# Fold products over four PSUM banks, weight loads issued first, and a reordered start of the first image

## The chip, the cores and the metric

The kernel runs on one NeuronCore of a Trainium2 chip. The metric is the device time of one execution in microseconds. Five runs of the kernel before took 671.73 to 672.25 us, with a median of 672.01 us.

The engines are named as the profile names them: PE is TensorE (PEld is its weight load), DVE is VectorE, ACT is ScalarE, POOL is GpSimd, and SP is SyncE, which here only issues transfers. PSUM is the memory that TensorE writes its products to; it has banks of 512 fp32 words for each partition.

## The reference

The input `x` is 4 images of 256 channels and 64 x 64 pixels, in fp32. Two layers follow each other. The first computes weights for 49 shifted copies of an image from the image itself, and sums the copies with these weights:

```python
k = conv(x, w1, padding=6, rhs_dilation=2) + b1       # w1: 128 x 256 x 7 x 7
k = conv(k, w2) + b2                                  # w2: 49 x 128 x 1 x 1
attn = softmax(k, axis=1)                             # over the 49 shifts
shifts = stack([xp[:, :, 2*u:2*u+64, 2*v:2*v+64] for u in range(7) for v in range(7)], axis=1)
x = einsum('bkchw,bkhw->bchw', shifts, attn)
```

The second whitens the channels in 4 groups of 64: mean and covariance over all images and pixels, five Newton-Schulz steps on the 64 x 64 covariance, the product with the centred data, then gain and shift for each channel.

## The kernel before

Nothing non-linear stands between the two convolutions, so the kernel multiplies their weights first: `w2 * w1` is one 7 x 7 convolution from 256 channels to 49 maps, and `w2 * b1 + b2` its bias. I call this product the fold. Channels come in two halves of 128 (`cc` in the code, `NCC = 2`).

**The prologue.** SP's queue issues, in program order: w2 (line 169), b1 (171), b2 twice (175), then w1 in five pieces for each half of the channels (`w1_sb`, line 215; pieces of 30, 30, 30, 20 and 18 channels), then the first image (225), then gain and shift (233, 234). The first image comes in 16 loads of 256 KB. It is split by row parity (`pr`, one buffer for each), by half of the channels, and by phase `a`, the row number modulo 4 within a parity; the order of the phases is 3, 0, 1, 2.

TensorE transposes w2 (182), DVE copies it twice into `w2T` (184), and a product with b1 (186) gives the bias (188). Then the fold follows: 13 blocks of 10 channels (the last of 8). A block is one fp32 product for each half (line 251, 490 columns, written to partitions 0 to 48 and 64 to 112 of one PSUM bank), and one eviction of both (`evict`, line 244). The profile shows an fp32 product as two records, which I call passes. Blocks alternate between the two banks `cv_buf`, and evictions between ACT (even blocks) and DVE (odd blocks). The evicted fold lies with output maps on partitions; 49 transposes (269), in 13 groups of 4 in the `tp` banks, turn it to have channels on partitions, and the same `evict` moves each group to `tap`, again by turns of ACT and DVE.

**The convolution.** It is done in the manner of Toom-Cook (Winograd) in both directions. Rows and columns are split into four phases, and weights and image are evaluated at seven points in each direction (`ROWS`, `BANKS`). The point 0 and the point at infinity of the rows are done as direct convolutions (`direct`, line 779), the others as products of evaluated weights and evaluated image (`conv_bank`, line 604), whose results are interpolated on DVE.

For the first image the order of the work on DVE is written out by hand (`in_turn`, `strict`): each DVE instruction is kept behind the one before in the program. The part that matters here is: `row_weights(1)` adds weight taps (into `lgx`, then `gbr`), `weights` evaluates them for the columns into `wr`, `row_eval(0, 1)` adds image phases (0 + 2 into `rb[0]`, 1 + 3 into `rb[1]`, for each parity, then both into `rb[2]`), and `col_ops` evaluates the columns into `ct` and `xh`. At the same time TensorE does `direct0(INF, 0)`, which reads phase 3 of the image, and `direct0(0, 0)`, which reads phase 0; then it begins with `conv_bank` for rows of point 1, which reads `wr` and `xh`. Program order on TensorE is kept by `pe(...)`.

**Behind it.** The other three images follow in the same way, with softmax, the weighted sum of shifted pixels (products with `band` matrices that go through DRAM, lines 1158, 1208 and 1328), and the covariance sums (`sig`, line 1419) in planned gaps between convolution steps. The tail computes the whitening matrix and writes the output (lines 1730 to 1872). `acc` (line 820) are two more PSUM banks, of the pool that later holds the weighted sums; DVE clears them (822) and the direct convolutions of the first image write to them. `diag` and `cmask` (117 to 126) are small constants for the softmax.

These lines are `evict`, the loop of the fold and the sums of phases in `row_eval`:

```python
    def evict(k, o, i):
        (nc.vector.tensor_copy if k % 2 else nc.scalar.copy)(o, i)

    for k, c0 in enumerate(range(0, P, CB)):
        n = min(CB, P - c0)
        t = cv_buf[k % 2]
...
            if br == 1:
                add(r[0], xs[:, 0], xs[:, 2])
                add(r[1], xs[:, 1], xs[:, 3])
```

Of the kernel before, what the change touches and what calls it, by code (L numbers as in the profile page):

```python
# [32 lines left out]
def kernel(  # L33
# [75 lines left out]
    def tp():  # L109
# [8 lines left out]
    diag = const.tile([P, SW + 2 * R], F32, name="diag")  # L118
    nc.gpsimd.memset(diag, 0.0)
    nc.vector.tensor_reduce(  # L120
        diag[:, R : R + SW], ident.rearrange("p (j w) -> p w j", w=SW), AX.X, ALU.add
    )
    cmask = const.tile([P, KS], F32, name="cmask")
    for v in range(KS):
        nc.vector.tensor_reduce(
            cmask[:, v : v + 1], diag[:, KS - 1 - v : KS - 1 - v + SW], AX.X, ALU.add
        )
# [41 lines left out]
    nc.sync.dma_start(w2_sb, w2.rearrange("k o a b -> k (o a b)"))  # L169
# [10 lines left out]
    nc.gpsimd.memset(w2T, 0.0)  # L180
    t = tp()
    nc.tensor.transpose(t[:O1, :KT], w2_sb, ident[:KT, :KT])
    for h in range(2):
        nc.vector.tensor_copy(w2T[:, h * HB : h * HB + KT], t[:O1, :KT])
    t = tp()
    nc.tensor.matmul(t[:, :1], w2T, b1_sb, start=True, stop=True)
    bias = const.tile([P, 1], F32, name="bias")
    nc.vector.tensor_tensor(bias, t[:, :1], b2_sb, ALU.add)

    cv_buf = []  # L190
    for k in range(2):
        t = ps_cv.tile([P, 512], F32, name=f"cv{k}")
        nc.vector.memset(t, 0.0)
        cv_buf.append(t)
    sig = ps_sg.tile([P, NCC, GW + 1], F32, name="sig")

# [9 lines left out]
    w1_sb = [w1p.tile([O1, P, KT], F32, name=f"w1_{cc}") for cc in range(NCC)]  # L206

# [3 lines left out]
    CB = 10  # L211
    for c0, c1 in ((0, 3), (3, 6), (6, 9), (9, 11), (11, 13)):
        c0, c1 = c0 * CB, min(c1 * CB, P)
        for cc in range(NCC):
            nc.sync.dma_start(
                w1_sb[cc][:, c0:c1].rearrange("o c t -> o (c t)"),
                w1[:, cc * P + c0 : cc * P + c1].rearrange("o c u v -> o (c u v)"),
            )
# [27 lines left out]
    for k, c0 in enumerate(range(0, P, CB)):  # L246
        n = min(CB, P - c0)
        t = cv_buf[k % 2]
# [11 lines left out]
        )  # L260
    every = [u * KS + v for u in UPOS for v in range(KS)]
    flat = tap.rearrange("p u v a k -> p (u v) a k")
    TB = 4
    for k0 in range(0, KT, TB):
        n = min(TB, KT - k0)
        t = tp()
        for k in range(n):
            pe(
                nc.tensor.transpose(  # L269
                    t[:, k * P : k * P + K2], tapT[:K2, every[k0 + k]], ident[:K2, :K2]  # L270
                )
            )
# [215 lines left out]
    def row_eval(b, br, rb=rb):  # L488

        for pr in range(2):  # L490
# [329 lines left out]
    acc = [ps_y.tile([P, Q8, W], F32, tag="y", name=f"acc{sr}") for sr in range(2)]  # L820
    for a in acc:
        nc.vector.memset(a, 0.0)
# [1083 lines left out]
```

## Time and profile before

| what | value |
| --- | --- |
| runs, median (lowest to highest) | 672.01 us (671.73 to 672.25) |
| the profiled execution | 677.36 us |
| its span, from first to last instruction | 675.6 us |
| PE busy | 648.5 us, 96% of the span |
| DVE busy | 566.5 us, 84% |
| ACT busy | 333.1 us, 49% |
| POOL busy | 115.3 us, 17% |
| DMA | 126.09 MB, 187 GB/s in the mean |
| mean granted TensorE clock | 0.989 |

The profile of one execution answers several questions. The page gives busy shares, the span in 40 slices of 16.9 us (each digit is a busy share in tenths), and the chain of work that ended last, followed back from the end. A row of the timeline has its start in us, its duration, the engine, the source line, the operation with the tile that it writes and those that it reads, the shape, and the number of merged instructions; in brackets stand the idle time before it and what ended it. A row of the waits reads: who waited, for whom, us in total, times, longest. A row of the table by stretches has the stretch, its length, then busy us (and the number of instructions) of PE, PEld, DVE, ACT and POOL, then the granted clock of TensorE as a share of full speed, the busy share of the DMA engines and GB/s. Where no clock event is recorded before a stretch, the table shows 1.00.

### The profile page before, as it was taken

To read this page: it belongs to the slowest core of one execution; us is meant where nothing else is said; L and a number is where in the kernel's file an instruction comes from. 1 tells how busy PE (TensorE), PEld (TensorE's weight loads), DVE (VectorE), ACT (ScalarE), POOL (GpSimd) and SP (SyncE) were. 2 spreads that over 40 slices of the span, in tenths; PEclk is the share of its full clock that TensorE was granted. 3 is DMA by queue.
4 is the path that set the end of the run, shared out by engine and by line. 5 is a ranking of instruction groups with operands and counts; after the bars stand their busy time and mean duration, and the time that the engine had idled before them with its cause. 6 is when DMAs were issued, how large, how long until landed. Compare 5 with 4: busy or idle time off the path is not lost.

```text
span 675.6 us, 19064 instructions
## 1 busy us (share of the span) xinstructions
PE 648.5 (96%) x7800; PEld 529.1 (78%) x7800; DVE 566.5 (84%) x1240; ACT 333.1 (49%) x862; POOL 115.3 (17%) x173
## 2 busy tenths in 40 slices
PE   6999999999999997999999999999999999999993
PEld 1439573357899996989999999899999999998430
DVE  3699999999399889979999879989999988633773
ACT  1424331023565564556756464455754476635663
POOL 0000551662213011000122020002130203400000
PEclk9999999999999998999999999999999999999997
DMA  8951899994599979412668594026374334749698
GB/s 315 250 166 66 134 250 370 218 191 59 118 208 223 193 260 310 120 51 80 179 221 294 173 320 120 2 67 170 105 195 117 75 71 105 193 96 383 247 405 346
DMA packets 110991, 126.09 MB, mean 187 GB/s; under 512 B 69255, under 2 KB 92344, under 8 KB 109752
## 3 DMA queue, kind: packets, MB, share of 16 engines
q1 hardware_dynamic: 94104, 69.35, 35.8%
q0 software_dynamic: 10752, 37.26, 21.4%
q10 hardware_dynamic: 6048, 18.27, 9.1%
q8 instruction: 61, 1.00, 0.6%
q14 instruction: 26, 0.21, 0.1%
HBM read 78.78 MB, written 52.36 MB: 194 GB/s over the span
## 4 chain that ended last, share of the span: by engine, by line
PE 85%; DMA 6%; DVE 5%; ACT 1%; issue 1%; SPq 0%; POOL 0%; DVEq 0%; ACTq 0%; POOLq 0%
PE cv L604 30%; PE y L1328 14%; PE cv L779 12%; PE acc L779 8%; PE sig L1419 5%; PE tp L1400 4%; PE tp L1264 4%; DMA out_dram<-out 3%; DMA slot<-in_x_dram 3%; PE cv L251 2%; PE tp L1730 1%; PE tp L1021 1%; PE tp L269 1%; DVE pv L352 1%; DMA w<-in_L_conv_w_dram 1%
## 5 line engine op out<-in xcount | busy, mean ns | idle before, releaser
L604 PE MATMUL cv<-xh,wr 128*49 128x128 f32 x4160 | 233.5, 274 | 0.1
L604 PEld LDWEIGHTS cv<-xh,wr 128*49 128x49 f32 x4160 | 227.3, 124 | 3.2 <-issue 1.0
L1158 POOL DMA_DIRECT2D sd<-zt x120 | 63.3, 534 | 300.4 <-ACT zt L1139 237.6
L1328 PE MATMUL y<-band,xb 128*128 128x209 f32 x448 | 93.7, 341 | 0.4 <-ACT xb L1295 0.4
L1328 PEld LDWEIGHTS y<-band,xb 128*128 128x128 f32 x448 | 75.7, 191 | 1.3 <-ACT xb L1295 0.6
L615 ACT COPY pv<-cv 113x486 f32<-113x486 f32 (+2 forms) x60 | 25.9, 432 | 86.6 <-PE cv L604 82.6
L352 DVE SCALAR_TENSOR_TENSOR pv<-pv 113x162 f32<-113x162 f32 x176 | 53.5, 326 | 1.5 <-ACT pv L615 0.9
L1410 ACT COPY yt<-tp 128x512 f32<-128x512 f32 x60 | 34.9, 589 | 24.8 <-PE tp L1400 23.9
L1139 ACT COPY zt<-d 32x112 f32<-32x112 f32 (+2 forms) x132 | 38.6, 292 | 11.1 <-DVE d L1009 5.7
L1400 PE MATMUL tp<-ident,slot 128*128 128x128 f32 x240 | 41.3, 296 | 0.2 <-ACT slot L1350 0.2
L1264 PE MATMUL tp<-ident,slot 128*128 128x128 f32 x256 | 40.9, 284 | 0.0
L1061 ACT ACTIVATE d<-tp,mx 128x49 f32<-128x49 f32 x96 | 27.5, 323 | 26.5 <-DVE mx L1058 19.8
L1419 PE MATMUL sig<-yt 128*64 128x65 f32 x1024 | 38.0, 225 | 0.9 <-ACT yt L1410 0.9
L1400 PEld LDWEIGHTS tp<-ident,slot 128*128 128x128 f32 x240 | 34.9, 205 | 5.1 <-issue 3.6
L1264 PEld LDWEIGHTS tp<-ident,slot 128*128 128x128 f32 x256 | 38.5, 205 | 0.4 <-DMA sd<-zt 0.4
L1419 PEld LDWEIGHTS sig<-yt 128*64 128x64 f32 x1024 | 32.9, 137 | 6.7 <-issue 1.9
L1295 ACT COPY xb<-tp 128x512 f32<-128x512 f32 x52 | 30.6, 588 | 9.1 <-PE tp L1264 6.0
L779 PE MATMUL acc<-slot,tap 128*49 128x256 f32 (+7 forms) x224 | 34.7, 468 | 0.0
L352 DVE SCALAR_TENSOR_TENSOR xh<-ct 128x512 f32<-128x512 f32 x40 | 26.6, 696 | 6.2 <-PE cv L604 5.9
L779 PEld LDWEIGHTS acc<-slot,tap 128*49 128x49 f32 x224 | 16.1, 123 | 17.9 <-issue 15.5
L147 POOL DMA_DIRECT2D slot<-in_x_dram x12 | 20.4, 1701 | 54.4 <-DVE xh L352 38.3
L348 DVE TENSOR_TENSOR pv<-pv 113x162 f32<-113x162 f32 (+1 forms) x77 | 27.8, 370 | 0.3
(258 smaller groups left out, 1143.9 us busy)
## 6 DMA issues: line engine op xcount, KB each, us to landing
out_dram<-out SPq DMA_DIRECT2D x31, 512.0 KB, 5.2
band<-sd SPq DMA_DIRECT2D x64, 242.0 KB, 3.2
sd<-zt POOLq DMA_DIRECT2D x120, 77.0 KB, 4.1
wr<-gd ACTq DMA_DIRECT2D x14, 588.0 KB, 4.2
wr<-gd ACTq DMA_DIRECT2D x14, 490.0 KB, 4.3
slot<-in_x_dram POOLq DMA_DIRECT2D x12, 512.0 KB, 10.5
ahead<-in_x_dram POOLq DMA_DIRECT2D x12, 512.0 KB, 7.5
spill<-slot POOLq DMA_DIRECT2D x3, 2048.0 KB, 8.2
```

The source lines that it names most:

```text
L348: return in_turn(TT(o, a, b, ALU.subtract))
L352: return in_turn(STT(o, a, f, b, ALU.mult, ALU.add))
L604: nc.tensor.matmul(o, wv[:, sc, sr, cc], xv[bc][:, h * NCC + cc], start=(j == 0), stop=(j == len(terms) - 1), skip_group_check=True,)
L779: nc.tensor.matmul(ps[h * HB : h * HB + KT, :, o0:o1], w[v][:, cc], rhs, start=(j == 0 and k == 0), stop=(j == len(order) - 1), skip_group ...
L1139: ins = nc.scalar.copy(o, i)
L1158: dma = queue.dma_start(bass.AP(tensor=D.tensor, offset=D.offset + h * HS + g * RS, ap=[[LS, TC], [CR * RS, NCH], [1, KS * WS]],), zt[p0 : ...
L1264: nc.tensor.transpose(t[:, h * C + cc * P : h * C + (cc + 1) * P], tile_of(xt, cc, t8, h, pc), turned_by(n),)
L1295: (nc.vector.tensor_copy if n > 4 * B - 3 else nc.scalar.copy)(xb.rearrange("p a c -> p (a c)"), t[:, : 2 * C])
L1328: nc.tensor.matmul(y_ps[n, half, cc][:, q0 : q0 + nq, c0:c1], xb[:, cc * P : (cc + 1) * P], rhs, start=(k == 0), stop=(k == len(PIECES[hal ...
L1400: nc.tensor.transpose(t[:, h * C + cc * P : h * C + (cc + 1) * P], tile_of(yt, cc, t8, h, pc), turned_by(n),)
L1410: return nc.scalar.copy(yb.rearrange("p h a g c -> p (h a g) c")[:, :, :GW], t[:, : 2 * C].rearrange("p (e c) -> p e c", c=GW),)
L1419: nc.tensor.matmul(sig[g * GW : (g + 1) * GW, cc], yb[:, g, :GW], yb[:, g], start=(count[0] == 0), stop=end, skip_group_check=True,)
```

## The change

It has six edits, all ahead of or inside the first image's start.

1. w1's loads are issued first on SP's queue, in six pieces for each half (10, 20, 30, 30, 30 and 8 channels); b1 and b2 follow them there, and w2 is issued on ACT's queue.
2. Five products of the identity with itself (`warm`) stand around the transpose of w2, and TensorE's program order now holds from there.
3. The fold rotates over four banks, `cv_buf` and `acc`. `acc` is made and cleared in the prologue for this, behind the copies of `w2T`.
4. The bias product stands behind the fold; `diag` and `cmask` are made behind the copies of `w2T`.
5. Of the 13 groups of transposes DVE evicts four (1, 3, 6 and 9), ACT nine.
6. The first image's phases are loaded in the order 3, 0, 2, 1, and for row point 1 the sums of phases 1 + 3 come behind the sums 0 + 2 of both parities.

On POOL only the clearing of `diag` moves, behind the identity. After these steps each engine has the same instructions in the same order as before.

```diff
-    nc.sync.dma_start(w2_sb, w2.rearrange("k o a b -> k (o a b)"))
+    nc.scalar.dma_start(w2_sb, w2.rearrange("k o a b -> k (o a b)"))
+    w1_sb = [w1p.tile([O1, P, KT], F32, name=f"w1_{cc}") for cc in range(NCC)]
+
+    CB = 10
+    for c0, c1 in ((0, 1), (1, 3), (3, 6), (6, 9), (9, 12), (12, 13)):
+        c0, c1 = c0 * CB, min(c1 * CB, P)
+        for cc in range(NCC):
+            nc.sync.dma_start(
+                w1_sb[cc][:, c0:c1].rearrange("o c t -> o (c t)"),
+                w1[:, cc * P + c0 : cc * P + c1].rearrange("o c u v -> o (c u v)"),
+            )
...
+    def warm(n):
+
+        t = tp()
+        for _ in range(n):
+            pe(nc.tensor.matmul(t[:, :P], ident, ident, start=True, stop=True))
+
+    warm(2)
     t = tp()
-    nc.tensor.transpose(t[:O1, :KT], w2_sb, ident[:KT, :KT])
+    pe(nc.tensor.transpose(t[:O1, :KT], w2_sb, ident[:KT, :KT]))
     for h in range(2):
-        nc.vector.tensor_copy(w2T[:, h * HB : h * HB + KT], t[:O1, :KT])
-    t = tp()
-    nc.tensor.matmul(t[:, :1], w2T, b1_sb, start=True, stop=True)
-    bias = const.tile([P, 1], F32, name="bias")
-    nc.vector.tensor_tensor(bias, t[:, :1], b2_sb, ALU.add)
+        w2_turned = nc.vector.tensor_copy(w2T[:, h * HB : h * HB + KT], t[:O1, :KT])
+    warm(3)
...
+    acc = [ps_y.tile([P, Q8, W], F32, tag="y", name=f"acc{sr}") for sr in range(2)]
+    for a in acc:
+        with tc.issue_after(w2_turned.ins):
+            nc.vector.memset(a, 0.0)
...
-    for c0, c1 in ((0, 3), (3, 6), (6, 9), (9, 11), (11, 13)):
...
-    for a in (3, 0, 1, 2):
+    for a in (3, 0, 2, 1):
...
-        t = cv_buf[k % 2]
+        t = (*cv_buf, *(a.rearrange("p q w -> p (q w)") for a in acc))[k % 4]
...
+    t = tp()
+    pe(nc.tensor.matmul(t[:, :1], w2T, b1_sb, start=True, stop=True))
+    bias = const.tile([P, 1], F32, name="bias")
+    nc.vector.tensor_tensor(bias, t[:, :1], b2_sb, ALU.add)
...
         evict(
-            k0 // TB, flat[:, k0 : k0 + n],
+            k0 // TB in (1, 3, 6, 9), flat[:, k0 : k0 + n],
...
+        odd = []
...
             if br == 1:
                 add(r[0], xs[:, 0], xs[:, 2])
-                add(r[1], xs[:, 1], xs[:, 3])
+                odd.append((r[1], xs[:, 1], xs[:, 3]))
...
+        for o in odd:
+            add(*o)
```

More of the change, by code (lines that the diff above doesn't have):

```diff
@@ L116 @@
     nc.gpsimd.tensor_copy(ident3[:, P:], ident[:, :GW])
[L118 to L127, printed above, removed]
     pivot = const.tile([P, NCC], F32, name="pivot")
@@ L194 @@
         cv_buf.append(t)
+    acc = [ps_y.tile([P, Q8, W], F32, tag="y", name=f"acc{sr}") for sr in range(2)]
+    for a in acc:
+        with tc.issue_after(w2_turned.ins):
+            nc.vector.memset(a, 0.0)
     sig = ps_sg.tile([P, NCC, GW + 1], F32, name="sig")
+    diag = const.tile([P, SW + 2 * R], F32, name="diag")
+    nc.gpsimd.memset(diag, 0.0)
+    with tc.issue_after(w2_turned.ins):
+        nc.vector.tensor_reduce(
+            diag[:, R : R + SW], ident.rearrange("p (j w) -> p w j", w=SW), AX.X, ALU.add
+        )
+    cmask = const.tile([P, KS], F32, name="cmask")
+    for v in range(KS):
+        nc.vector.tensor_reduce(
+            cmask[:, v : v + 1], diag[:, KS - 1 - v : KS - 1 - v + SW], AX.X, ALU.add
+        )
     NSK = 2 * NCC * KT
@@ L205 @@
     gb5 = gpool.tile([P, KS, NCC, 2, KT], F32, name="gb5")
-    w1_sb = [w1p.tile([O1, P, KT], F32, name=f"w1_{cc}") for cc in range(NCC)]
     tapT = w1p.tile([P, KT, P], F32, name="tapT")
-    CB = 10
-    for c0, c1 in ((0, 3), (3, 6), (6, 9), (9, 11), (11, 13)):
[L213 to L218, printed above, removed]
     for pr in range(2):
         slots[pr] = store[pr]
-    for a in (3, 0, 1, 2):
+    for a in (3, 0, 2, 1):
         for pr in range(2):
@@ L818, in direct_start @@
         direct(1, 0, sr, conv_psum(), [gr0[:, v, :, sr] for v in range(KS)])
-    acc = [ps_y.tile([P, Q8, W], F32, tag="y", name=f"acc{sr}") for sr in range(2)]
-    for a in acc:
-        nc.vector.memset(a, 0.0)
     rows = [(0, br) for br in (1, 2, 3)]
```

## The prediction, made before the result was known

> **What bounds the kernel now.** I read the page first (slices, then the chain), then the timeline of the first 60 us, the DMA rates of the first 45 us, the waits of the first 29 us, and last a table of TensorE by stretch and the chain around 250 us.
>
> ```profile
> PE   6999999999999997999999999999999999999993
> PE 85%; DMA 6%; DVE 5%; ACT 1%; issue 1%; SPq 0%; POOL 0%; DVEq 0%; ACTq 0%; POOLq 0%
> ```
>
> TensorE is the bound, and it is full nearly everywhere. It stops for long at three places: the first slice, slice 16 (a stall near 265 us) and the last one. The change works in the first. All five engines' instruction orders, before against after, differ only in the prologue (up to the first image's row sums), so what is won or lost there is handed on if TensorE stays without gaps behind it.
>
> The timeline of TensorE and of the queue that loads:
>
> ```profile
> 2.33 6.58 SPq L215 DMA_DIRECT2D w<-in_L_conv_w_dram  x10
> 6.70 15.66 PE L251 MATMUL cv<-w,w2T 128*49 128x490 f32 x52 [1.97 <-DMA w<-in_L_conv_w_dram]
> 20.68 0.17 PEld L251 LDWEIGHTS cv<-w,w2T 128*49 128x49 f32 x2 [0.16 <-DMA w<-in_L_conv_w_dram]
> 22.41 0.49 ACT L244 COPY tapT<-cv 113x392 f32<-113x392 f32 x1 [1.40 <-PE cv L251]
> 22.95 3.44 PE L269 MATMUL tp<-ident,tapT 113*128 113x113 f32 x32 [0.58 <-ACT tapT L244]
> 26.57 1.79 PE L269 MATMUL tp<-ident,tapT 113*128 113x113 f32 x16 [0.19 <-ACT tap L244]
> 28.53 0.32 PE L269 MATMUL tp<-ident,tapT 113*128 113x113 f32 x1 [0.17 <-ACT tap L244]
> 28.78 11.59 PE L779 MATMUL cv<-slot,tap 128*49 128x512 f32 x56
> ```
>
> Fold products run from 6.70 to 22.4, tap transposes to 28.8, then convolution without a gap. The third line is the one that matters: the last fold weights land at 20.68 - 0.04 = 20.64 and TensorE was already there. The waits of the first 29 us and the DMA rates (40 slices of 1.125 us):
>
> ```profile
> PEld cv L251 <- DMA w<-in_L_conv_w_dram: 4.1, 4, 2.1
> PEld cv L251 <- DVE tapT L244: 3.6, 5, 0.8
> PEld cv L251 <- ACT tapT L244: 3.3, 6, 0.7
> GB/s 0 22 1 136 397 403 408 423 413 429 418 423 418 411 429 412 405 320 232 218 218 217 218 218 228 216 193 203 214 237 228 219 189 218 145 157 389 393 392 149
> ```
>
> The eviction waits (6.9 us) look like the prize of four banks. They are not: the weights (6.42 MB) flow at about 415 GB/s from 4.1 to 19.7 without a break, so the fold is load-bound at its end, and a faster TensorE would wait for data instead.
>
> **The change part by part.**
>
> *Weights first.* The first weight load moves from 2.33 to the queue's first slot, 0.75 (where w2 is issued now): 1.58 us earlier at equal latency. In the slices data starts about 4.1, 1.8 us after issue, and w2, issued at 0.75, is used at 2.54; small b1/b2 loads now sit directly ahead, so part of the 1.8 may be theirs, which would make the gain 2.2. On the other side a first piece of 245 KB lasts 0.6 us and an issue takes 0.43 us at the median (0.33 to 0.71), so a gap of up to 0.6 us can open: gain 1.0. I take 1.7, near the plain move. w2 goes out on ACT's queue; ACT's first eviction comes only at 10.5 us, so its table load (1.28 us) behind that issue has room.
>
> *Pieces.* The last piece is 8 channels, but the one ahead has 30, and its second half decides. All lands at 20.64 - 1.7 = 18.94; the two last halves are 2 x 196 KB = 0.40 MB, 0.97 us, so the second half of channels 90 to 119 is there at 17.97. TensorE then owes blocks 9 to 12 of that half. The two halves go to separate output partitions and run side by side, so a half alone takes as long as a whole block: from the direct convolution, 56 passes in 11.59 us are 0.207 us each, 0.41 for two side by side; so 0.82 us for both passes of a 490-column block. Three blocks, then a 0.33 us pass (392 columns) and a last record of 0.49: 3 x 0.82 + 0.33 + 0.49 = 3.28. Start 18.01, end 21.29, against 22.37 now: 1.08 gained, 0.6 less than the loads gain.
>
> *Four banks.* They keep those blocks free of evictions; evictions run at 0.57 (ACT) and 0.67 (DVE), each for every second block (1.64). With two banks the same burst would wait about 0.2 us per block, so 0.5. The accumulators' memsets (1.03) move onto DVE after w2T, over 1 us before block 2.
>
> *Warm-up.* Records of 1022 to 1055 ns until 12, against 574 from 13, show half rate at the start. Two passes alone took 1.87 there (6.70 to 8.6), so five identity products of 128 columns are 5 x 1.87 x 128/490 = 2.4 us, while TensorE waits for data; the last three may hold the first block up by a microsecond: 0 at the end. A cold block costs 1.64 against 1.22 of load, so the fold may fall some four blocks behind by 10 us; it catches up at 0.82.
> The Trainium skill ("TensorE: Matmul & The Clock Gate", Part 1) says that full clock comes after a busy window of 3.4 us that runs freely, whatever the instruction count; by it the warm-up alone is too short, and the sum would stay the same, since loads set the end. "DMA: Bandwidth & Descriptors" (Specifications) puts HBM at about 358 GB/s for a core; by it the weights would need 17.9 us, but the slices show 397 to 429, and they decide.
>
> *The bias product* moves behind the fold, where TensorE waits 0.58 us for the last eviction (now two records, 0.58 at half rate): hidden, if b1, now behind the weights, has landed. It lands about 19.5, used at 21.3.
>
> *Transposes.* 13 groups of 0.39 are 5.1 us; they take 5.83 (22.95 to 28.78). Two waits of about 0.35 each (26.57, 28.53) come from ACT. Nine evictions on ACT (0.57 apart, 5.1) and four on DVE free DVE for its row sums; replaying the groups by hand with three buffers I lose about 0.25 instead of 0.7. Gain 0.45; bounds -0.3 (nine ACT evictions become the stream) and 0.7.
>
> *Image loads and sums.* 16 loads of 256 KB at 218 GB/s, 1.2 us each, follow the weights; with b1/b2 between (0.5) they move up by 1.2. Phase order 3, 0, 2, 1 and odd sums last:
>
> ```profile
> 38.16 4.63 DVE L345 TENSOR_TENSOR rb<-slot 128x1024 f32<-128x1024 f32 x4 [1.24 <-DMA slot<-in_x_dram]
> 48.22 1.23 DVE L352 SCALAR_TENSOR_TENSOR ct<-rb 128x1024 f32<-128x1024 f32 x1
> 51.57 8.68 PE L604 MATMUL cv<-xh,wr 128*49 128x128 f32 x156
> 93.22 2.29 DVE L352 SCALAR_TENSOR_TENSOR rb<-rb,rb 128x2048 f32<-128x2048 f32 x1
> 97.00 2.30 PE L779 MATMUL acc<-rb,gbr 128*49 128x512 f32 x10
> ```
>
> The 1.24 us wait goes: the even sums find their data; the last odd sum needs the 16th load, about 40.5 - 1.2 = 39.3, ends 40.5 instead of 42.8. DVE gains 2.3, but TensorE does not wait for it: xh is ready 3.4 us before 51.57. It is cover, not gain. DVE is full from 52 to 97, so this cover passes down: at 97.00 TensorE uses what DVE finished at 95.51, 1.5 us earlier. If DVE gained nothing, the first 1.5 us would still pass there.
>
> **Sum.** 1.08 + 0.45 = 1.53, with a little for the slow tail of the last load (it shares the queue with the image): 1.6. The profiled execution took 677.36 (span 675.6); it should take 675.8. The median of the runs, 672.01, lies 5.35 below that; the same loss gives 670.4. Bounds: load 1.0, transposes -0.3: 0.1; load 2.2 and 0.7: 2.4. About 0.2%, 1.3 us, is what a measurement can tell.
>
> **The place where this can change size.** At 265:
>
> ```profile
> 247.87 17.20 DMA slot<-in_x_dram
> 267.08 1.17 PE y L1328 x4
> 264.60:268.00 3.40, 0.92 (x4) 0.93 (x5) 3.23 (x6) 2.51 (x5) 0.00 (x0) 0.51 0.68 227
> 268.00:271.50 3.50, 3.50 (x30) 3.13 (x31) 3.46 (x7) 3.14 (x5) 0.00 (x0) 0.50 0.77 276
> 271.50:275.00 3.50, 3.50 (x68) 3.50 (x66) 3.43 (x7) 0.18 (x1) 0.00 (x0) 1.00 0.05 16
> ```
>
> TensorE idles 4.62 us and then works at a granted clock of 0.5 until 271.5: 4.4 us, 2.2 lost. The idle stretch moves up by 1.6 with the work. If the clock still rises at 271.5, 6.0 us run at half rate (3.0 lost, 0.8 worse); if it rises half of the 6.9 us step earlier, at 268.05, 1.3 are lost (0.9 better). I can't tell which, and the forecast leaves the loss as it is.
>
> **Rivals.**
> 1. Forecast, 670.4: 0.50; its own range 669.6 to 671.5.
> 2. The clock rises earlier behind the stall: 669.5, 0.18. For: TensorE would be busy for three quarters of that stretch instead of a quarter.
> 3. It rises at the same time: 671.2, 0.17. For: a busy half (6.70 to 8.6 of 5.2 to 8.6) did not lift it at the start.
> 4. The gain does not reach the end, or the change does not do what it says: bank waits turn into load waits, loads start no earlier, or the stall at 265, of which 17.2 us are a transfer, keeps its time: 672.0, 0.08. Against: that transfer is issued behind bands that follow TensorE's own work.
> 5. Slower: the clock stays at half through the fold's end. Then the last four blocks cost 3 x 1.64 + 0.65 + 0.82 = 6.4 instead of 3.28: -1.6 + 3.1 = +1.5, 673.5, 0.07. It decides if the clock is not up by about 14 us (five cold blocks by 12, four fast ones after, are still in time at 18). Against: cold, TensorE is slower than the loads and so never idle, as from 8.6 to 12 when it rose.
>
> **How the numbers follow.** Faster by over 0.2%: rival 1 two thirds (0.33), rival 2 nearly all (0.17), rival 3 a little (0.03): 0.53. Slower: 0.07. The rest 0.40. Range 668.7 to 672.2: from rival 2 with the better bound of the loads to rival 4.
>
> **What would show it.** First weight load at 0.75; last fold wait on a weight load at about 18, with four blocks after it; transposes from 21.9; convolution from 27.2; even row sums without a wait; first L604 about 50.0; the gap near 265 at 261 to 265.5. It is wrong if TensorE waits for DVE between 50 and 97, or if fold products still end after 22.

## The result and the profile after

The changed kernel takes 673.18 us in the median of 54 executions (671.83 to 679.38), the kernel before 671.98 us in 94 (671.62 to 678.17). The ratio is 1.0032, with a 95% interval of 1.0019 to 1.0045: **slower by 0.3%, where 670.4 was forecast.** The time is outside the range, and on the side that had 7%.

The executions of each kernel fall in two groups, and the difference has two parts. 77 of before's 94 lie at 671.62 to 672.56 us (median 671.95), 17 at 676.36 to 678.17. Of the changed kernel's 54, 31 lie at 671.83 to 674.03 (median 672.72), 23 at 677.10 to 679.38. So the changed kernel loses 0.77 us where nothing special happens, and it is in the upper group more often. Both profiled executions, 677.36 us before and 677.57 after (span 675.8), are of the upper group, so their profiles can be compared with each other, but both show a loss that most executions don't have.

The page after, TensorE's slices and the shares of the chain of work:

```profile
PE   8999999999999997999999999999999999999993
PE 82%; DMA 8%; DVE 6%; ACT 1%; issue 1%; SPq 1%; DVEq 0%; ACTq 0%
```

The first slice went from 6 to 8, though nothing became faster: the warm-up's identity products are in it. What counts is on the chain: DMA went from 6% to 8%, TensorE from 85% to 82%. The timeline of the first 53 us (start, length, engine, line, and in brackets the idle time and what ended it):

```profile
0.75 8.33 SPq L166 DMA_DIRECT2D w<-in_L_conv_w_dram  x12
4.75 1.88 PE L261 MATMUL cv<-w,w2T 128*49 128x490 f32 x4
7.49 2.34 PE L261 MATMUL cv<-w,w2T 128*49 128x490 f32 x3 [0.86 <-DMA w<-in_L_conv_w_dram]
...
19.63 0.61 PE L261 MATMUL cv<-w,w2T 128*49 128x490 f32 x1 [0.77 <-DMA w<-in_L_conv_w_dram]
...
22.89 0.38 PE L272 MATMUL tp<-b_sb,w2T 128*128 128x1 f32 x2
23.54 5.68 PE L283 MATMUL tp<-ident,tapT 113*128 113x113 f32 x49 [0.26 <-ACT tapT L254]
29.14 11.59 PE L796 MATMUL cv<-slot,tap 128*49 128x512 f32 x56
36.93 4.63 DVE L359 TENSOR_TENSOR rb<-slot 128x1024 f32<-128x1024 f32 x4
```

The loads go out at 0.75 instead of 2.33, and the first fold product starts at 4.75 instead of 6.70. But the wait for the second half of the 30-channel piece (channels 90 to 119) ends at 19.63, and the convolution starts at 29.14, 0.36 us later than before (28.78). DVE's row sums start at 36.93 without a wait (38.16 before, after 1.24 of waiting). The DMA rates of the first 45 us, in slices of 1.125 us (first the engines' busy tenths, then GB/s):

```profile
DMA  0298699999999999999999999989999999759992
GB/s 0 50 354 239 171 343 387 382 413 418 429 423 429 418 429 408 357 270 198 236 208 220 218 220 222 236 156 220 215 262 220 215 220 215 86 208 402 395 388 80
```

Data starts earlier and then falls to 239 and 171 GB/s from 3.4 to 5.6 us; it needs until 9 us to be back above 400. Before, it ran at 397 GB/s and more from 4.5 us on. This stretch uses up the whole head start. The chain of work through it:

```profile
3.08 0.43 SPq L166
...
5.81 13.78 DMA w<-in_L_conv_w_dram
19.59 0.04 issue
19.63 0.61 PE cv L261
```

The decisive piece, issued at 5.81, lands at 5.81 + 13.78 = 19.59. The slow stretch is no want of issued loads: the issue at 3.08 is the sixth, so by 3.51 loads of 3.0 MB had been issued, while by 3.4 us 0.45 MB had moved.

### The profile page after: what moved, and what is told of

The parts are those of the page before. It is cut to its first block, busy times and chain, and to the rows that moved or that the text cites. A ratio compares the mean times of both kernels' runs of the same rounds, so it can differ in the third digit from the quotient of the medians.

```text
span 675.8 us, 19093 instructions
## 1 busy us (share of the span) xinstructions
PE 651.3 (96%) x7810; PEld 531.4 (79%) x7810; DVE 566.0 (84%) x1238; ACT 333.2 (49%) x864; POOL 115.0 (17%) x173
## 4 chain that ended last, share of the span: by engine, by line
PE 82%; DMA 8%; DVE 6%; ACT 1%; issue 1%; SPq 1%; DVEq 0%; ACTq 0%
PE cv L621 30%; PE y L1342 14%; PE cv L796 12%; PE acc L796 8%; PE sig L1433 4%; PE tp L1414 4%; PE tp L1278 4%; DMA out_dram<-out 3%; DMA slot<-in_x_dram 3%; DMA w<-in_L_conv_w_dram 2%; PE tp L1744 1%; PE tp L1035 1%; SPq L166 1%; DVE pv L366 1%; PE cv L1744 1%
## 5 line engine op out<-in xcount | busy, mean ns | idle before, releaser
L1342 PE MATMUL y<-band,xb 128*128 128x209 f32 x448 | 93.7, 341 | 0.1
L1342 PEld LDWEIGHTS y<-band,xb 128*128 128x128 f32 x448 | 75.7, 191 | 1.0 <-issue 0.6
```

The costliest lines, as they stand in the source:

```text
L1342: nc.tensor.matmul(y_ps[n, half, cc][:, q0 : q0 + nq, c0:c1], xb[:, cc * P : (cc + 1) * P], rhs, start=(k == 0), stop=(k == len(PIECES[hal ...
```

## The experiments

For each run: the start of the convolution in its profile (us), the median and number of executions, the ratio to before with its 95% interval, and how many executions took over 675 us. Before has 28.78 there, the changed kernel 29.14.

| run | convolution | median, n | ratio [95%] | over 675 |
| --- | --- | --- | --- | --- |
| loads_only | 27.06 | 670.38, 9 | 0.9976 [0.9967, 0.9985] | 0 |
| after_old_pieces | 26.63 | 670.62, 11 | 0.9986 [0.9973, 0.9999] | 1 |
| after_old_loads | 28.44 | 672.09, 12 | 1.0013 [0.9998, 1.0029] | 2 |
| after_first30 | 27.27 | 671.55, 10 | 1.001 [0.9982, 1.0038] | 3 |
| after_20first | 27.67 | 671.02, 1 | | 0 |
| after_two_queues | 27.99 | 671.01, 1 | | 0 |
| after_10_30 | 28.95 | 676.08, 7 | 1.0046 [1.0025, 1.0068] | 4 |
| loads_phase | 27.58 | 670.28, 9 | 0.9977 [0.9967, 0.9986] | 0 |
| after_no_phase | 26.92 | 670.25, 12 | 0.9985 [0.997, 0.9999] | 1 |
| after_fill | 29.26 | 680.05, 6 | 1.0118 [1.0098, 1.0139] | 6 |
| after_again | 28.60 | 676.72, 1 | | 1 |
| before_again | 28.73 | 671.85, 1 | | 0 |
| after_pool_copy | 28.27 | 677.95, 9 | 1.0085 [1.006, 1.011] | 9 |
| after_early_x | 29.44 | 673.21, 10 | 1.0032 [1.0019, 1.0046] | 2 |
| loads_fine_tail | 27.06 | 670.27, 8 | 0.9969 [0.995, 0.9988] | 0 |
| best_mix | 26.11 | 670.33, 12 | 0.9991 [0.9978, 1.0005] | 0 |
| after_two_queues_timed | 28.38 | 671.20, 12 | 0.9994 [0.9975, 1.0013] | 2 |
| after_fine_tail | 26.61 | 669.82, 12 | 0.9977 [0.9957, 0.9996] | 1 |

Behind the start of the convolution, the 14 profiled executions of less than 675 us all take 641.21 to 642.11 us to the end of their span, and the four with the loss near 265 us (both kernels, after_again, after_old_loads) take 646.32 to 647.27. So where that loss is absent, the time follows the head. (after_fill and after_pool_copy, which change the work near 265 us, stand apart.)

**Is the head start lost because loads go first, or because of the pieces?** Two theories: A, a transfer that starts earlier ends no earlier, whatever the pieces; B, the new list of pieces is what moves slowly at the head.

loads_only is the kernel before with the weight loads first in the old pieces, w2 on ACT's queue and the bias product behind the fold:

```diff
-    nc.sync.dma_start(w2_sb, w2.rearrange("k o a b -> k (o a b)"))
+    nc.scalar.dma_start(w2_sb, w2.rearrange("k o a b -> k (o a b)"))
+    for c0, c1 in ((0, 3), (3, 6), (6, 9), (9, 11), (11, 13)):
...
```

> The kernel before with one edit: w1's loads first on SP's queue in the old pieces (30, 30, 30, 20, 18 channels), w2 on ACT's queue, b1 and b2 behind w1 and the bias product behind the fold. Theory A (the head start is lost in the first microseconds of the loads, whatever the pieces): the last weights still land at 20.3 to 20.7, convolution starts at 28.6 to 28.9, time within 0.3 us of before. Theory B (the small first pieces starve the DMA engines): with old pieces data runs at 400 GB/s from about 2.6, the last weights land at about 19.1, convolution starts near 27.5, and the executions are 1.0 to 1.3 us shorter than those of before of the same clock.

after_old_pieces is the changed kernel with one line edited:

```diff
-    for c0, c1 in ((0, 1), (1, 3), (3, 6), (6, 9), (9, 12), (12, 13)):
+    for c0, c1 in ((0, 3), (3, 6), (6, 9), (9, 11), (11, 13)):
```

> The changed kernel with the old pieces of w1 (30, 30, 30, 20, 18 channels). Theory A: last weights land at 20.3 to 20.7 as in both kernels, but three blocks and not four stand behind them, so the fold ends 0.6 us earlier than in the changed kernel (22.4) and convolution starts near 28.5. Theory B: last weights at about 18.9, fold ends near 20.6, convolution near 26.8, 2 us under before at the same clock.

The DMA rates of loads_only:

```profile
GB/s 0 62 248 413 423 429 423 423 434 418 423 392 422 409 404 389 204 240 222 219 230 214 221 224 223 151 222 234 236 230 225 216 213 49 346 389 392 340 6 0
```

Above 400 GB/s from the fourth slice on, without a dip; the convolution starts 1.72 us earlier than before (27.06), and the time is 1.52 us lower (670.38 against 671.90 run side by side). after_old_pieces starts it at 26.63 and takes 670.62. Theory A falls, B stands: the gain that the prediction saw in the loads is there with the old pieces. The median of after_old_pieces gains only 1.28 us of the 2 that B expected; its profiled execution, 669.95, gains them, but the ten without the loss spread over 1.0 us.

after_old_loads is the reverse: the changed kernel with before's loads, pieces and their place (the bias product stays behind the fold).

> The changed kernel with w2, b1, b2 and w1 loaded as before; four banks, warm-up products, transposes' evictions and the image's phases stay changed. Both theories: last weights land at 20.6; four banks then save at most 0.3 in the last blocks and the new split of evictions 0.2, so convolution starts at 28.2 to 28.6 and the time is 0.2 to 0.6 under before at the same clock. If the four banks or the warm-up products cost something by themselves, convolution starts after 28.8.

The convolution starts at 28.44, so the four banks and the transposes together give 0.34 us; 672.09 us can't be told from before.

**Which piece is it?** The new list differs at both ends: it begins with 10 and 20 channels, and it ends with 30 and 8 instead of 20 and 18. Four kernels take this apart; each is the changed kernel with the list, or the queue, edited:

```diff
after_first30:    ((0, 3), (3, 6), (6, 9), (9, 12), (12, 13))
after_20first:    ((0, 2), (2, 4), (4, 6), (6, 9), (9, 12), (12, 13))
after_10_30:      ((0, 1), (1, 4), (4, 7), (7, 10), (10, 12), (12, 13))
after_two_queues:
-            nc.sync.dma_start(
+            (nc.sync, nc.scalar)[cc].dma_start(
```

> The changed kernel, with its two first pieces (10 and 20 channels) joined to one of 30 as in the old list; the new end (30 channels, then 8) stays. It separates the two ends of the new list. Theory B2 (the slow head comes from the small first pieces, and the last 30-channel piece costs the 0.6 us that the prediction gave it): weight data runs at about 420 GB/s from 3 us on without the dip to 200, all weights land near 18.5 instead of 20.1, the second half of the last 30-channel piece near 18.0 instead of 19.6, fold products end near 21.4, the convolution starts near 27.2 (changed kernel 29.1, with the old pieces 26.6), and executions without the 5 us loss near 265 us take about 670.9 (old pieces 670.6, changed kernel 672.7). Rival B3 (the new end of the list is what is slow, the head only lies beside it): the dip goes, but the convolution starts at 28.5 or later and the time stays above 672.

In after_first30, the rates, and the timeline of TensorE:

```profile
GB/s 0 80 272 418 423 418 429 418 439 423 423 418 418 418 396 339 185 226 221 231 248 233 212 225 195 183 213 227 245 239 213 219 211 28 381 397 384 306 16 0
```

```profile
17.76 0.61 PE L261 MATMUL cv<-w,w2T 128*49 128x490 f32 x1 [0.75 <-DMA w<-in_L_conv_w_dram]
...
21.67 5.67 PE L283 MATMUL tp<-ident,tapT 113*128 113x113 f32 x49 [0.26 <-ACT tapT L254]
27.27 11.59 PE L796 MATMUL cv<-slot,tap 128*49 128x512 f32 x56
```

The new end is kept, the dip is gone, and the times are those of the prediction (last wait 18.01, transposes 21.9, convolution 27.2). The new end costs 27.27 - 26.63 = 0.64 us against the old pieces. Theory B2 holds, B3 falls. The median of this run is pulled up by 3 of 10 executions over 675 us and one at 674.24; the other six lie at 670.79 to 671.66.

> The changed kernel with first pieces of 20, 20 and 20 channels instead of 10, 20 and 30; for the weight data of the first 8 us only. Theory B (every piece below 30 channels moves slowly at the head): 200 to 350 GB/s until the 20-channel pieces are through, near 5 us, weights landed near 19.2, convolution near 28.2. Rival B4 (only the 10-channel first piece starts the slow stretch): no stretch below 380 GB/s after 3 us, weights landed near 18.3, convolution near 27.3.

> The changed kernel, all pieces as they are, with the loads of the second half (cc = 1) issued on ScalarE's queue behind w2 instead of all twelve on SyncE's. For the weight data of the first 8 us only. Rival B5 (the dip comes from issuing twelve loads at 0.43 us and more on one queue): the dip to 200 GB/s goes, data at 400 GB/s or more from 3 us on, weights landed near 18.3. Theory B (the packets themselves are slow at the head, 0.3 us on average and up to 1.3 for 3920 bytes against 0.15 later, while all 16 engines are busy): the dip stays, and weights land at 19.3 or later.

> The changed kernel with weight pieces of 10, 30, 30, 30, 20 and 8 channels on the one queue: the small first piece is kept, the 20-channel piece behind it is not. Theory B6 (a 10-channel first piece on one queue starts the slow stretch, whatever follows): data at 200 to 300 GB/s between 3.5 and 6 us, weights landed at 19.3 or later. Rival B7 (it takes the second small piece too): no stretch below 380 GB/s after 3.5 us, weights landed near 18.4, convolution near 26.7 to 27.2.

The rates of these three, in this order:

```profile
GB/s 0 77 273 408 418 418 404 411 437 416 418 413 423 413 410 356 204 250 212 235 202 202 247 232 195 204 205 226 235 235 223 211 224 48 193 408 344 400 127 15
```

```profile
GB/s 0 39 332 396 434 420 415 439 418 418 418 418 417 411 413 343 212 254 210 224 222 217 219 227 219 133 204 196 254 235 221 217 218 77 364 390 399 314 4 15
```

```profile
GB/s 0 52 345 286 293 335 277 387 392 429 423 423 423 413 416 404 315 242 214 197 225 204 250 225 228 191 203 172 233 269 218 219 217 213 150 2 346 397 404 323
```

Three 20-channel pieces show no dip, though twelve loads stand on one queue: what I expected of theory B ("every piece below 30 channels moves slowly") falls, and B4 holds. With the 10-channel piece first and 30s behind it, rates of 277 to 335 GB/s last until 8 us: B6 holds, B7 falls. And the changed kernel's own pieces on two queues show no dip either, as B5 said. So the slow stretch needs **a first piece of 10 channels with all loads behind it on the same queue**; either one alone doesn't do it. Why the queue is then slow for some 4 us isn't settled. The engines were busy only 8 and 6 tenths in the two worst slices of the changed kernel, and 6 tenths at 171 GB/s is less per busy engine than 9 at 418: transfers are both thinner and slower there. In after_again, the same kernel, the engines are busy throughout most of the dip, so there the packets themselves are slow:

```profile
DMA  0399979999999999999999999979899999899980
GB/s 0 61 330 275 265 268 385 382 429 423 423 418 429 423 423 413 350 250 219 224 217 218 218 218 225 223 120 214 201 263 222 226 216 217 94 343 396 394 330 8
```

By the traces' packet records, packets of 3920 bytes took 253 ns in the mean from 3.4 to 5.6 us in the changed kernel (up to 1325), 230 in after_again, and 154 in after_20first.

The Trainium skill ("DMA: Bandwidth & Descriptors", Bandwidth) advises transfers of 1 MiB and more for three quarters of the peak, beside a table of transfers issued by GpSimd. It speaks against every piece here: a half of 10 channels is 245 KB, of 20 channels 490 KB, of 30 channels 735 KB. The runs bear it out only at the smallest first piece, and there only on one queue; 490 KB pieces moved at 404 to 418 GB/s.

**Do the other edits cost something?** Executions of the changed kernel without the loss take 0.77 us more, the convolution of the profiled one starts 0.36 us later. Theory P puts the rest on the first image's phase order and sums. loads_phase is loads_only with these added; after_no_phase is after_old_pieces with them put back:

```diff
-    for a in (3, 0, 1, 2):
+    for a in (3, 0, 2, 1):
...
-                add(r[1], xs[:, 1], xs[:, 3])
+                odd.append((r[1], xs[:, 1], xs[:, 3]))
```

> loads_only (weights first in the old pieces, bias product behind the fold) with the changed kernel's order of the first image's row phases and its odd sums last. Theory P (this order brings the extra 0.4 us and the wider spread of the changed kernel's executions, by the work that DVE and the loads then do at other times): median 670.7 to 671.0 against 670.38 for loads_only, spread of 0.8 us or more, some executions 5 us longer. Rival P2 (phase order is cover and nothing else, as the prediction had it): 670.2 to 670.5, spread like loads_only's 0.5.

> after_old_pieces with the old order of the row phases and sums put back, so that the rotation over four banks, the warm-up, the split of evictions and the loads first remain. Theory P: median 670.0 or less (670.38 of loads_only less the 0.4 us by which its convolution starts earlier), spread of about 0.5 us, no execution above 672. Rival P3 (the four banks or the warm-up bring the spread): 670.5 to 670.8 and a spread of 1 us, like after_old_pieces.

670.28 against loads_only's 670.38, and 670.25 against after_old_pieces' 670.62 with overlapping executions (669.93 to 670.93 without the loss there, 669.96 to 671.00 here). In loads_phase P falls by the median: the order is neither gain nor loss, as the prediction had it; the spread, 0.80 us against 0.53, is nearer to P. For after_no_phase neither expectation is met cleanly, since the spread of 1 us stayed.

**What is lost near 265 us?** Theory C was that the clock's fall behind TensorE's wait makes the upper group, so that filling the wait would cure it. after_fill adds identity products ahead of the product that waits:

```diff
+        if m[0] == "z" and n == 2 and half == 0:
+            t = tp()
+            for _ in range(16):
+                pe(nc.tensor.matmul(t[:, :P], ident, ident, start=True, stop=True))
```

> The changed kernel with 16 products of the identity (3.4 us of TensorE, results unused) set into TensorE's order where it stands idle near 262 to 267. Theory C (the executions of either kernel fall in two groups, near 672 and near 677.5, by whether the granted clock falls in this idle stretch, and the change makes the fall more frequent): no execution near 677.5 is left, all lie at 672 to 673.2 with a mean clock of 0.994 or more. Rival D (the 5 us are a late transfer and the clock only follows): both groups stay.

It takes 677.00 to 682.12 us, five of six executions more than the median of either kernel's upper group. In the profiled execution (677.00) the fill runs from 262.10 for 3.73 us, the product behind it starts at 265.67, no longer waiting, and the clock stays at 1.00. Still it takes 645.67 us behind the start of the convolution, some 4 more than executions without the loss. So the fill costs by itself, and this run can't part C from its rival. Two more profiles of the unchanged kernels can:

> The kernel before as it is, once more, for a profile of its more frequent kind of execution (about 672.0). Theory S: convolution starts near 28.8, the gap near 265 us is about 1.1 us instead of 4.6, the load of image 2 behind the band loads is issued near 243.3 instead of 247.9, and the clock stays at 1.0 there. Rival: the gap is 4.6 us here too, so that it isn't what parts the two kinds of execution.

> The changed kernel as it is, once more, for a second profile. Theory S with theory B: if this execution takes about 672.7, the head shows the same dip to about 200 GB/s between 3.5 and 6.5 us and the convolution starts near 29, but the image-2 load near 241 to 247 us is issued earlier than 246.99, TensorE's gap near 265 is about 1.1 us and the clock does not fall there. If it takes about 678, the profile repeats the first one (gap 4.6 us, clock 0.5 until 271).

before_again took 671.85 us, one of the lower group. The stretches of before_again, and of the changed kernel (third from the end stands the granted clock):

```profile
261.00:264.60 3.60, 2.49 (x25) 2.05 (x25) 3.43 (x7) 3.54 (x6) 0.00 (x0) 1.00 0.99 372
264.60:268.00 3.40, 3.40 (x68) 3.40 (x64) 3.30 (x5) 1.94 (x4) 0.00 (x0) 1.00 1.02 382
268.00:271.50 3.50, 3.50 (x52) 3.32 (x49) 3.50 (x6) 1.98 (x5) 0.00 (x0) 1.00 0.53 147
```

```profile
261.00:264.60 3.60, 1.53 (x8) 1.20 (x8) 3.53 (x7) 0.55 (x2) 0.00 (x0) 1.00 0.96 341
264.60:268.00 3.40, 0.71 (x3) 0.71 (x4) 3.23 (x5) 2.36 (x4) 0.00 (x0) 0.50 0.62 199
268.00:271.50 3.50, 3.50 (x29) 3.13 (x30) 3.47 (x6) 3.29 (x5) 0.00 (x0) 0.51 0.74 261
```

The wait itself is most of what parts the groups, so C falls. The product with `bandz` (L1328 before, L1342 after) waits 1.11 us in before_again and 4.76 in the changed kernel's profile:

```profile
262.87 0.69 PE L1328 MATMUL y<-bandz,xbz 128*128 128x96 f32 x4 [1.11 <-ACT xbz L1286]
```

```profile
267.29 1.17 PE L1342 MATMUL y<-bandz,xbz 128*128 128x96 f32 x4 [4.76 <-ACT xbz L1300]
```

SP's queue shows where it comes from, before_again first, then the changed kernel:

```profile
232.50 2.89 SPq L482 DMA_DIRECT2D gd<-wr  x1
...
242.07 0.97 SPq L1208 DMA_DIRECT2D band<-sd  x2
243.08 0.58 SPq L147 DMA_DIRECT2D slot<-in_x_dram  x1
```

```profile
232.89 4.01 SPq L496 DMA_DIRECT2D gd<-wr  x1
...
244.86 2.09 SPq L1222 DMA_DIRECT2D band<-sd  x2
246.99 1.31 SPq L137 DMA_DIRECT2D slot<-in_x_dram  x1
```

Issues on this queue take longer in the second, and the last of the four loads of image 2's even rows goes out at 246.99 instead of 243.08. It then takes 18.35 us:

```profile
246.99 18.35 DMA slot<-in_x_dram
265.35 0.02 issue
265.37 0.04 ACTq L525
265.40 0.04 issue
265.44 0.13 ACT rb L525
```

ACT's copy of image 2's row phase 0 (L525) waits for it, and the `xbz` copies for which TensorE waits stand behind that copy in ACT's queue. By the trace's semaphore counts, 15 of the load's 16 parts were in at 257.25 and the last at 265.35; in before_again all 16 were in at 254.98. Why one part is so late is open. after_again, of the upper group (676.72), repeats it: issue at 246.79, wait 4.65, half clock for 3.4 us. All 20 profiles fit. In the four with a wait of 4.55 to 4.76 us (both kernels, after_again, after_old_loads) the issue of `gd` near 232 takes 3.89 to 4.01 us and the last load goes out at 246.79 to 248.34. In the 14 others with this order of issues it takes 1.50 to 3.58 us, the load goes out at 240.62 to 243.23, and, fill and GpSimd copy apart, the wait is 1.08 to 1.11. The two with the image loads moved (after_early_x, best_mix) wait 1.11 and 1.10. Two kernels try to take this away; the first gives the copy to GpSimd, the second puts the four loads one step earlier on SP's queue:

```diff
after_pool_copy:
-                nc.scalar.copy(r[2], xs[:, 0])
+                (nc.gpsimd.tensor_copy if b == 2 else nc.scalar.copy)(r[2], xs[:, 0])
after_early_x:
-    for j in range(2, 6):
+    for j in (2, 2, 3, 4):
         plan(1, j, lambda: behind_band(next(pieces)))
```

> The changed kernel, with the copy of image 2's row phase 0 (128x1024 per half) given to GpSimd instead of ScalarE; nothing is left out. Theory S (the 5 us that about 4 in 10 executions of the changed kernel lose near 265 us come from ScalarE's queue: that copy waits for the late image-2 load, and the xbz copies that TensorE needs stand behind it): no execution is above 675, all lie between 671.8 and 673.8 like the faster group of the changed kernel, the granted clock of all is 0.994 or more, and TensorE has no gap above 1.5 us near 265. Rival S2 (the load is needed soon after by others too, or GpSimd's own issues now stand behind the waiting copy): executions above 676 stay about as frequent, or the gap moves to a wait on DVE or on band loads.

> The changed kernel with the four loads of image 2's first row half put one step earlier into SyncE's queue (the last one goes out where the third went, near 230 us, ahead of the band loads that hold it up near 241 to 247); nothing is left out. Theory S3 (the 5 us near 265 us that part the two kinds of execution are lost because this last load stands in SyncE's queue behind issues whose time varies, 243.1 against 246.8 to 247.9 us in the profiles, and ScalarE's copy waits for it): no execution above 675, all between 671.8 and 674, the last image-2 load has landed by about 245, TensorE's gap near 262 us stays at 1.1 us, no clock below 1.0 there. Rival S4 (SyncE's queue is late as a whole, and the band and weight loads behind it hold up TensorE just as long): executions above 676 stay at some 4 in 10, with another line in front of the gap.

after_pool_copy: all nine executions are over 676, so S falls as I put it and S2 has it. In its profile the load goes out early, at 242.38, and the wait near 261 is gone altogether, but two others came:

```profile
260.57 2.44 POOL L525 COPY rb<-slot 128x1024 f32<-128x1024 f32 x1 [2.62 <-issue]
262.14 1.48 DVE L359 TENSOR_TENSOR ct<-zz 113x576 f32<-113x576 f32 x1
...
292.23 1.76 PE L1342 MATMUL y<-band,xb 128*128 128x209 f32 x4 [3.28 <-ACT xb L1309]
```

DVE's sum beside GpSimd's copy takes 1.48 us (0.76 for the same shape right behind it), DVE is late from there, and TensorE waits 3.28 us at 292 and 2.0 at 331, each time with half a clock behind it. after_early_x: 2 of 10 executions over 675, against 23 of 54. That is not none, and too few to be called fewer, so neither S3 nor S4 is met; the executions without the loss did not gain.

How often the loss comes, counted as executions over 675 us: 28 of 62 with the 10-channel piece first on one queue (the changed kernel and after_10_30), 8 of 85 with loads first in larger pieces or on two queues, 23 of 226 with before's loads; runs that change the place near 265 are left out. Run side by side it was 23 of 54 against before's 17 of 94, and 4 of 7 against 1 of 29. These are safer than the sums, for before itself had 17 of 94 beside the changed kernel and 4 of 119 beside the experiments. So the loss comes more often with the slow head, but not only with it: after_first30 has it in 3 of 10. Through which transfers a head that is later by tenths of a microsecond reaches SP's queue at 232 us was not found.

**Is there a better version?** The experiments ask for large pieces first and small ones last:

```diff
loads_fine_tail (from loads_only), after_fine_tail (from the changed kernel):
+    for c0, c1 in ((0, 3), (3, 6), (6, 9), (9, 11), (11, 12), (12, 13)):
best_mix: after_fine_tail with the edit of after_early_x
```

> loads_only with the last 38 channels as 20, 10 and 8 instead of 20 and 18: the finer tail without any other edit. With two banks the burst at the end goes at the pace of the evictions; after the last half lands (18.4) one pass is left instead of two. Fold end 0.2 to 0.5 us earlier, convolution near 26.7, time 669.9 to 670.3. If evictions set the end, nothing changes: 670.4.

> The changed kernel with weight pieces of 30, 30, 30, 20, 10 and 8 channels (a head of large pieces, a tail of small ones) and the image-2 loads one step earlier; nothing is left out. By theories B2 and S3 together: weight data at about 420 GB/s from 3 us on, all landed near 18.3, of the last 30-channel piece nothing is late, the fold is left with blocks 11 and 12 after the second half of channels 100 to 109 lands near 17; fold end near 20.2, convolution from about 26.3 (old pieces 26.6), time 669.6 to 670.5 with no execution above 675. If it is above 670.9, the finer tail costs what it saves.

> The changed kernel, every piece as it is, with the loads of the second half (cc = 1) issued on ScalarE's queue, now timed. Theory B5/B6 (the slow stretch needs the 10-channel piece and all loads on one queue): data above 400 GB/s from 3.5 us in this profile too, convolution near 28.0, executions without the loss near 265 us at 670.8 to 671.3, and if that loss goes with the late head, at most 2 in 10 executions above 675. Rival: the one profile was luck, the stretch of 200 to 300 GB/s is back and the time 672.7.

> The changed kernel with weight pieces of 30, 30, 30, 20, 10 and 8 channels, the image-2 loads left where they are. Convolution from about 26.2, time 669.6 to 670.2 for executions without a loss. If the group 3 us higher that best_mix showed (5 of 12) came from the moved image-2 loads, it is gone here; if it comes from the pieces, 4 in 10 executions lie at 672.6 to 673.5 again.

The finer tail alone changes nothing at the end (27.06 again, 670.27), though its fold ends 0.42 us earlier, with the bias product at 20.16 instead of 20.58. Its transposes:

```profile
20.84 0.99 PE L269 MATMUL tp<-ident,tapT 113*128 113x113 f32 x8 [0.30 <-ACT tapT L239]
22.03 2.64 PE L269 MATMUL tp<-ident,tapT 113*128 113x113 f32 x24 [0.19 <-ACT tap L239]
24.86 1.79 PE L269 MATMUL tp<-ident,tapT 113*128 113x113 f32 x16 [0.19 <-ACT tap L239]
```

They stop for ACT's evictions and give it back: the 16 start at 24.86 in loads_only too, where the transposes begin 0.39 later. With four banks and the new split of the evictions they take 5.60 us without a stop. after_fine_tail takes 669.82 us, nine of twelve at 669.41 to 670.29, and with an interval of 0.9957 to 0.9996 it beats the kernel before; beside the changed kernel it was not run. Its other three take 671.81, 674.11 and 675.04. best_mix has no execution over 675 but five of twelve at 672.64 to 673.50. after_fine_tail has none in that stretch and three others above the rest, so neither half of its expectation is met cleanly, and no profile here shows what these executions lose. Two queues bring the changed kernel to 671.20, with 2 of 12 over 675, which can't be told from before (0.9975 to 1.0013).

## Why the prediction was wrong

- **The loads, a gain of 1.7: this step failed.** The prediction took "a gap of up to 0.6 us can open" as the worst that the first piece could do, and kept the gain at 1.0 or more. The second half of channels 90 to 119 landed at 19.59 instead of 17.97, and 1.62 us of the 1.7 were gone. The gap was reckoned from issue times against bytes, with the rate of 415 GB/s behind it; no row of before had a first piece that small. What came was no gap between issues, but a stream of 171 to 387 GB/s from 3.4 to 9 us over loads already issued. The prediction's own sign of being wrong, fold products after 22, came with it. after_first30, with 17.72 there, shows that the rest of the step was right.
- The blocks after it, 3.28: right. In the changed kernel the fold ends at 22.98 (the eviction behind it starts at 23.00), 3.35 after 19.63. The 0.6 for the 30-channel piece next to last: right, 0.64.
- The four banks, 0.5: not seen. The transposes start 0.11 us earlier in after_old_loads than in before (22.84, 22.95) and 0.21 earlier in after_old_pieces than in loads_only (21.02, 21.23). No run has the changed kernel's pieces with two banks, so the burst for which the 0.5 was reckoned is untested.
- The transposes, 0.45: mis-sized. From their start to the convolution it takes 5.60 us instead of 5.83, a gain of 0.23.
- Image loads and sums as cover: right. The wait of 1.24 us went, DVE began 1.23 us earlier, and TensorE got nothing from it; loads_phase confirms it in time.
- The warm-up and the bias product, nothing: no run speaks against it. The clock was up at about 12 as before, so rival 5 has no part in the loss, and its 673.5 lies near the result by chance.
- The clock near 265: the two profiles agree with "leaves the loss as it is" (waits of 4.62 and 4.76, half clock until about 271.5 in both). But the step from profile to median, "the same loss gives 670.4", took for granted that the loss comes as often. It doesn't: the median of 673.18 lies 0.46 above that of the executions without it.

The sum: 29.14 - 27.2 = 1.94 us of head, 0.46 from the more frequent loss, together 2.40 of the 2.78 between 670.4 and 673.18. The 0.4 left is not settled. The five profiles with the changed head start the convolution at 28.27 (after_pool_copy), 28.60 (after_again), 29.14, 29.26 (after_fill) and 29.44 (after_early_x), those of before at 28.73 and 28.78. Of two executions without the loss, before_again and after_early_x (image loads moved), the second starts the convolution 0.71 later and ends 0.90 later. Since the rest takes nearly the same time in all executions without the loss, the 0.4 may be the head's own spread; the starts of the executions that were not profiled are not known.

## What to carry to other kernels

A smaller first piece brings the first product forward, but where the last byte decides, what counts is the rate of the whole stream: keep the pieces that the trace shows at full rate at the head, put the small ones last, and look at the GB/s row before believing in a head start. Before a profile's time is carried over to a median, ask whether the profiled execution is one of the many or one of the few, and take a second profile; a loss that came in 17 of 94 executions came in 23 of 54 after an edit 200 us ahead of it. A copy that waits for a transfer holds up everything behind it in its engine's queue, and a transfer that waits behind other issues on one queue is late by more than they are: here 4 us at issue became 10 at landing (254.98 and 265.35).

## What the runs showed of the hardware

- A first load of 245 KB, with eleven more behind it on one queue, brought the stream down to 171 and 239 GB/s (277 to 335 in after_10_30) and kept it below 400 until 9 us (10 in after_10_30); all six profiles with such a first load on one queue show the dip. The same pieces on two queues, or a first load of 490 KB, ran at 396 GB/s or more from the fourth slice (3.4 us) on.
- The clock fell after shorter waits than the one at 265. In after_pool_copy, a wait of 2.0 us that ended at 333.29 (granted clock third from the end):

```profile
329.00:331.30 2.30, 2.28 (x15) 2.04 (x13) 2.30 (x10) 0.70 (x2) 0.00 (x0) 1.00 0.86 253
331.30:333.10 1.80, 0.00 (x0) 0.00 (x0) 1.80 (x5) 0.45 (x1) 0.00 (x0) 1.00 0.63 209
333.10:336.50 3.40, 3.21 (x11) 3.03 (x12) 3.40 (x7) 2.75 (x8) 0.00 (x0) 0.51 0.51 148
```

In after_10_30, where the fold starved, TensorE was busy for 1.08 of 3.40 us, and the next 3.4 us went at half:

```profile
7.10:10.50 3.40, 1.08 (x4) 0.22 (x6) 0.00 (x0) 0.21 (x1) 0.00 (x0) 1.00 0.99 375
10.50:13.90 3.40, 3.40 (x10) 1.00 (x12) 0.67 (x1) 0.00 (x0) 0.00 (x0) 0.50 1.02 422
```

The waits of 1.1 us near 261 were not followed by it in any of the 14 profiles that have them. The Trainium skill ("TensorE: Matmul & The Clock Gate", Why this matters for your kernels) warns of idle gaps above about 3 us; here it fell after a wait of 2.0 us.
- The two copies of 128x1024 on GpSimd took 2.44 and 1.10 us, both partly beside DVE (ACT takes 1.04 and 1.05 in the changed kernel), and the DVE sums that overlapped them took 1.48 and 1.40 us instead of 0.76.
